# SBUF buffers by the draft's list schedule: a macaron of mixture of experts and routed attention on one core

## The chip, the cores and the metric

The kernel runs on one core of a Trainium2 chip. A core has TensorE (PE, matmuls into PSUM), VectorE (DVE), ScalarE (ACT), GpSimd (POOL) and SyncE (SP, which here issues DMAs); each takes its own instructions strictly in the order in which the program lists them, and semaphores tie the engines together. The metric is device time in microseconds from launch to end. Times are compared by the median of several runs.

## The reference

The input x holds 8 sequences of 1024 rows of 256 numbers. Three layers follow one another, each on a layer norm of its input and added to it:

```
x = x + 0.5 * ffn(layernorm(x))
x = x + attention(layernorm(x))
x = x + 0.5 * ffn(layernorm(x))
```

`ffn` is a mixture of 8 experts, 2 for each row: a router product and softmax choose two experts and their weights, and every expert is `gelu(x @ W1 + b1) @ W2 + b2` with 128 hidden units. `attention` has a light part, 8 heads of 64 in windows of 64 rows that look one window to each side, and a heavy part: two score vectors choose 256 rows for the queries and 256 for the keys of each sequence; these attend to each other fully, and the results are added at the chosen rows.

```
sim = einsum('bhnid,bhnjd->bhnij', qw * scale, kk)      # light: 64 queries, 192 keys
attn = softmax(where(valid, sim, neg))
light_out = einsum('bhnij,bhnjd->bhnid', attn, vv) @ wo_l
hattn = softmax(einsum('bhid,bhjd->bhij', hq * scale, hk))   # heavy: 256 by 256
```

## The kernel before, in words

**Two passes and a planner.** The kernel text (`program`) does not issue instructions. Each call on `nc.tensor`, `nc.vector` and the others records an `Op` (the recording line is L269, so most rows of the profile carry that line). `macaron` runs `program` twice: first as a draft, whose operations `Plan.order` puts into a list order per engine with a model of durations, and then again, emitting them in that order. Copies out of PSUM (`nc.copy`, called `evict`) and scalings may go to either of two engines; the planner chooses.

**How the order is made.** `edges` (L435) collects for each operation what must come before it: operations on the same data, and for buffers that are used again, the users of the earlier tenant. `schedule` (L517) is a list schedule: at every step it takes the engine that can start soonest and the best-ranked ready operation in a window of 40. `backward` (L633) gives ranks from the end; five rounds are run and the best kept.

**Buffers.** SBUF pools such as `two`, `three` and `wpool` hold a fixed count of buffers per tag; `Pool.tile` deals them out in turn in the order in which `program` asks, and `edges` makes all users of one tenant precede all users of the next tenant of that buffer. The four PSUM banks of the pool `pmm` are treated otherwise: `banked` (L319) hands out "loose" tiles, and `schedule` gives such a tile a bank when the first operation that uses it is placed, the bank that has been free for the shortest time. The draft's assignment is then used in the second pass.

**The stages.** `program` builds the work as generators and interleaves their steps by positions along a common axis; `PLACES` holds for each generator (by number) a shift of its start and of its end. The generators:

- `rows`: for a group of one or two sequences, normalise the rows, transpose them (pt), compute the router's logits (pl), rank them, and find a slot for each row in a list sorted by expert, padded to 128 rows per expert; store the rows (y).
- `experts` (L1145): for up to four slots of 128 rows at a time, gather rows (xp, GpSimd), fetch the slot's expert weights (wt, SP), transpose into pt, evict to turned rows xTe, multiply (ph), Gelu to act with 4 x 128 columns for four slots, multiply (po, after a small product that adds b2), evict to yp, and store it to ys.
- `dense` (L1271): for the first and the last sequence all 8 experts are computed for all rows, without gathering: ph, Gelu to act (512 columns for 4 row tiles in the first, 256 for 2 in the last), po, and a weighted sum into the rows on VectorE (x_0at, x_last). The last sequence's four chunks end the program. Each begins with its router: pl, a chain of small VectorE steps to the gate weights, parts, pt_w, turned, and pb.
- `front`, `heavy`, `project`, `light`, `last`: combine the experts' rows, choose rows for the heavy part with eight rounds of digits (pd), compute heavy and light attention, and sum up. A light block: `scores_light` writes sim, `soften` takes the maximum (nmax), exponentials with their sums (a, asum) on ScalarE, the reciprocal, and scales a on VectorE or GpSimd; `keys_first` (L1435) transposes a into pa and evicts it to at; `values_light` (L1523) does the same for pb and bt, multiplies with the values (pav), and evicts to loT, which the output product (lo) reads.

In names, `_2f` is a group of the experts, `_7f` the dense last sequence, `_5atl` light and `_5ath` heavy attention of sequence 5.

**Which buffers take turns.** xTe, yp, bt: two each. at: three. act: two of 4 x 128 columns.

Of the kernel before, what the change touches and what calls it, by code (L numbers as in the profile page):

```python
# [44 lines left out]
F32 = mybir.dt.float32  # L45
# [33 lines left out]
    1: (0.014, 0.072),  # L79
    2: (0.088, 0.002),  # L80
    3: (0.444, -0.124),
    4: (-0.157, -0.245),
    5: (-0.045, -0.526),
    6: (0.377, -0.016),
    8: (-0.109, 0.000),
    9: (0.160, -0.078),
    10: (0.002, -0.129),
    11: (0.070, 0.254),
    12: (0.003, 0.003),
    13: (0.434, 0.082),  # L90
    14: (0.122, -0.024),
    15: (0.274, 0.222),
    16: (0.214, 0.139),
    17: (0.169, 0.000),
    18: (0.273, -0.045),
    19: (0.099, 0.049),
    20: (0.074, -0.435),
    21: (0.000, 0.117),
    22: (0.205, -0.014),
    23: (-0.072, -0.036),  # L100
    24: (-0.039, -0.018),
    25: (-0.013, 0.000),
    26: (0.055, 0.481),
    27: (-0.013, 0.068),
    28: (-0.016, 0.000),
    30: (0.000, 0.002),
    31: (0.000, 0.484),
    32: (0.000, 0.090),
    34: (-0.002, 0.015),
    36: (0.063, 0.000),  # L110
    37: (0.034, -0.012),
    38: (0.032, 0.032),
    39: (0.000, -0.362),
    40: (0.029, 0.010),
    41: (0.499, 0.498),
    42: (0.099, 0.231),
    43: (0.000, 0.020),
    44: (0.050, -0.164),
    45: (0.007, -0.066),
    46: (0.311, 0.028),  # L120
    47: (0.196, 0.228),
    48: (0.076, -0.023),
    49: (0.030, -0.083),
    50: (0.000, 0.068),
    51: (-0.049, -0.114),
    52: (0.025, 0.137),
    53: (0.005, -0.060),
    54: (0.066, -0.609),
    55: (0.019, -0.108),
    56: (0.030, 0.183),  # L130
    57: (0.236, 0.070),
    58: (0.064, 0.043),
    59: (0.047, -0.286),
    60: (0.034, 0.000),
    61: (0.050, 0.000),
    62: (-0.041, -0.014),
    63: (0.123, -0.043),
    64: (-0.124, -0.048),
    65: (-0.290, -0.365),
    66: (-0.097, 0.030),  # L140
    67: (0.024, -0.106),
    68: (-0.011, 0.032),
    69: (0.132, 0.030),
    70: (0.439, 0.061),
# [144 lines left out]
class Plan:  # L289


    def __init__(self, tc, draft=None):
        self.tc, self.nc, self.ops = tc, tc.nc, []
        self.tag = {}
        self.draft = draft
        self.banks = 0
        self.loose = []
        for name in ENGINES:
            setattr(self, name, Engine(self, name))

    def pool(self, ctx, name, bufs, **where):

        made = ctx.enter_context(self.tc.tile_pool(name=name, bufs=1, **where))
        shared, count = name not in ("cons", "dram"), {}

        class Pool:
            @staticmethod
            def tile(shape, dtype, tag, name):
                if shared:
                    count[tag] = count.get(tag, -1) + 1  # L310
                    tag = f"{tag}.{count[tag] % bufs}"
                t = made.tile(shape, dtype, tag=tag, name=name)
                if shared:
                    self.tag[t.name] = tag
                return t

        return Pool

    def banked(self, ctx, name, bufs, **where):  # L319


        made = ctx.enter_context(self.tc.tile_pool(name=name, bufs=1, **where))
        self.banks, ready = bufs, {}

        def make(shape, dtype, tile_name, i):
            return made.tile(shape, dtype, tag=f"{name}.{i}", name=tile_name)

        if self.draft:
            for i, bank in self.draft.opened:
                shape, dtype, tile_name = self.draft.loose[i]  # L330
                ready[i] = make(shape, dtype, tile_name, bank)

        class Pool:
            @staticmethod
            def tile(shape, dtype, name):
                i = len(self.loose)
                self.loose.append((shape, dtype, name))
                if self.draft:
                    assert self.draft.loose[i] == self.loose[i]
                    return ready[i]  # L340
                t = make(shape, dtype, name, 0)
                self.tag[t.name] = i
                return t

        return Pool

# [88 lines left out]
    def edges(self):  # L435
# [42 lines left out]
        for i, users in enumerate(self.users):  # L478
            lo, hi = min(users), max(users)
            down, up = set(users), set(users)  # L480
            for k in range(lo, hi + 1):
                if not before[k].isdisjoint(down):
                    down.add(k)
            for k in range(hi, lo - 1, -1):
                if k in up:
                    up.update(q for q in before[k] if q >= lo)
            inside = users | (down & up)
            asked = set().union(*(before[k] for k in inside)) - inside
            self.asks[i] = len(asked)
            for k in asked:  # L490
                self.opens[k].append(i)
            for k in users:
                self.uses[k].append(i)
# [10 lines left out]
    def in_turn(self, before, result, bank_of):  # L504

        place = {k: i for i, (_, k, _) in enumerate(result)}
        before = [set(qs) for qs in before]
        lines = {}
        for i in sorted(range(len(bank_of)), key=lambda i: min(place[k] for k in self.users[i])):
            lines.setdefault(bank_of[i], []).append(i)  # L510
        for line in lines.values():
            for i, j in zip(line, line[1:]):
                for k in self.users[j]:
                    before[k].update(self.users[i])
        return before

    def schedule(self, before, after, rank):  # L517
# [18 lines left out]
        free_at = dict.fromkeys(range(self.banks), 0.0)  # L536
# [14 lines left out]
        def next_of(e):  # L551

            best, looked = None, 0
            for r, k in waiting[e]:
                how = ops[k].how
                t = max(now[e], ready[k] + SIGNAL[e])
                if self.uses[k]:
                    new = [i for i in self.uses[k] if i not in bank_of]
                    if new:
                        if not free_at or any(asks[i] for i in new):  # L560
                            continue
                        t = max(t, min(free_at.values()) + SIGNAL[e])
# [15 lines left out]
        while len(result) < len(ops):  # L578
            e = min((e for e in ENGINES if found[e]), key=lambda e: found[e][0])
# [27 lines left out]
            for i in self.uses[k]:  # L607
                if i not in bank_of:

                    bank_of[i] = max(  # L610
                        free_at,
                        key=lambda x: (free_at[x] <= t, free_at[x] if free_at[x] <= t else -free_at[x], -x),
                    )
                    del free_at[bank_of[i]]
                last_use[i] = max(last_use[i], done)
                left[i] -= 1
                if not left[i]:
                    free_at[bank_of[i]] = last_use[i]
            if self.opens[k] or self.uses[k]:
                stale.add(PE)  # L620
# [60 lines left out]
    def order(self):  # L681
# [6 lines left out]
        for _ in range(ROUNDS):  # L688
            from_end = self.backward(before, *this[1:])
# [32 lines left out]
def program(  # L722
# [23 lines left out]
    two = nc.pool(ctx, "two", 2)  # L746
    three = nc.pool(ctx, "three", 3)
# [397 lines left out]
    def experts(f, group, routed, results):  # L1145
# [5 lines left out]
        for q in range(0, NS, 4):  # L1151
# [4 lines left out]
            for j in range(0, here, 2):  # L1156
# [16 lines left out]
                pt = bank(f"pt_{m}")  # L1173
                for i in range(two_of):
                    for k in range(KD):
                        nc.tensor.transpose(pt[:, ts(2 * i + k, P)], xp[:, i, ts(k, P)], ident)
                xT = two.tile([P, 2, KD, P], F32, tag="xTe", name=f"xTe_{m}")
# [4 lines left out]
                hidden.append(ph)  # L1182
                for i in range(two_of):
                    for k in range(KD):
                        nc.tensor.matmul(
# [6 lines left out]
            act = two.tile([P, 4, P], F32, tag="act", name=f"act_{n}_{q}")  # L1192
            for i in range(here):
                nc.scalar.activation(act[:, i, :], hidden[i // 2][:, i % 2, :], AF.Gelu, bias=wt[i][:, WROW - 1 : WROW])
            for j in range(0, here, 2):
# [3 lines left out]
                po = bank(f"po_{m}")  # L1199
                for i in range(two_of):  # L1200
                    s = q + j + i
                    nc.tensor.matmul(
# [6 lines left out]
                    nc.tensor.matmul(  # L1209
                        po[:, ts(i, D)],  # L1210
                        act[:, j + i, :],
# [4 lines left out]
                yp = two.tile([P, 2, D], F32, tag="yp", name=f"yp_{m}")  # L1216
# [54 lines left out]
    def dense(rows_of, weights, n, yT=None):  # L1271
# [73 lines left out]
        for e in range(E):  # L1345
            flat = bank(f"ph_{n}_{e}")[:, : m * P]
            for k in range(KD):
                nc.tensor.matmul(
# [6 lines left out]
            act = two.tile([P, 4, P], F32, tag="act", name=f"act_{n}_{e}")  # L1355
            nc.scalar.activation(
                act.rearrange("p i c -> p (i c)")[:, : m * P], flat, AF.Gelu, bias=b1_sb[:, e : e + 1]
            )
            for j in range(0, m, 2):
                po = bank(f"po_{n}_{e}_{j}")  # L1360
                for i in range(2):
                    nc.tensor.matmul(
                        po[:, ts(i, D)],
                        act[:, j + i, :],
# [70 lines left out]
    def keys_first(a, starts, n):  # L1435

        pa = bank(f"pa_{n}")
        for i in range(4):
            k = slice(starts[i % 2], starts[i % 2] + P)
            nc.tensor.transpose(pa[:, ts(i, P)], a[:, i, k], ident)  # L1440
        at = three.tile([P, 4, P], F32, tag="at", name=f"at_{n}")
# [81 lines left out]
    def values_light(a, vside, t, g, loT, n):  # L1523
# [4 lines left out]
        pb = bank(f"pb_{n}_{g}")  # L1528
        for c in range(2):
            pair = a[:, 2 * c : 2 * c + 2, :].rearrange("p j k -> p (j k)")  # L1530
            nc.tensor.transpose(pb[:, ts(c, P)], pair[:, P : 2 * P], ident)
        bt = two.tile([P, 2, P], F32, tag="bt", name=f"bt_{n}_{g}")
# [603 lines left out]
```

## Time and profile before

| | us |
|---|---|
| median of 7 runs | 1834.31 |
| lowest, highest | 1825.64, 1849.82 |
| the profiled execution | 1839.09 |
| its span, first to last instruction | 1837.4 |
| TensorE busy | 1681.8 |
| VectorE busy | 1232.6 |
| ScalarE busy | 917.0 |
| GpSimd busy | 846.6 |
| mean granted TensorE clock | 0.962 |

A row of the profile names line, engine, operation, and the tiles written and read (`out<-in`), then busy time, the mean of one in ns, and the idle time of the engine just before, with what ended it. PEld is the loading of matmul weights, which overlaps PE. "issue" and "remote" are idle times for which the profile shows no releaser of its own. The chain is followed back from the last instruction to what released each step.

### The profile page before, as it was taken

To read this page: it belongs to the slowest core of one execution; us is meant where nothing else is said; L and a number is where in the kernel's file an instruction comes from. 1 tells how busy PE (TensorE), PEld (TensorE's weight loads), DVE (VectorE), ACT (ScalarE), POOL (GpSimd) and SP (SyncE) were. 2 spreads that over 40 slices of the span, in tenths; PEclk is the share of its full clock that TensorE was granted. 3 is DMA by queue.
4 is the path that set the end of the run, shared out by engine and by line. 5 is a ranking of instruction groups with operands and counts; after the bars stand their busy time and mean duration, and the time that the engine had idled before them with its cause. 6 is when DMAs were issued, how large, how long until landed. Compare 5 with 4: busy or idle time off the path is not lost.

```text
span 1837.4 us, 39317 instructions
## 1 busy us (share of the span) xinstructions
PE 1681.8 (92%) x13753; PEld 1255.4 (68%) x13753; DVE 1232.6 (67%) x3904; ACT 917.0 (50%) x2554; POOL 846.6 (46%) x733
## 2 busy tenths in 40 slices
PE   6899899999999998899989899989989998999997
PEld 5576577666766766667667576748757665678786
DVE  5778658863865485677556698649647695558746
ACT  1134446546755543555646345637637554455532
POOL 1054662563643225443555644456445635453433
PEclk8899999999999998999999989999999999999999
DMA  9467664244851235464775432537665525744264
GB/s 157 171 207 220 221 208 146 74 120 140 263 156 55 54 98 172 154 212 122 237 226 173 118 107 87 158 118 228 193 190 165 141 89 164 216 118 132 73 189 125
DMA packets 220134, 284.66 MB, mean 155 GB/s; under 512 B 53496, under 2 KB 160960, under 8 KB 219680
## 3 DMA queue, kind: packets, MB, share of 16 engines
q1 hardware_dynamic: 190992, 208.82, 36.7%
q0 software_dynamic: 28368, 73.31, 15.1%
q8 instruction: 109, 1.79, 0.4%
q14 instruction: 89, 0.73, 0.1%
q10 hardware_dynamic: 576, 0.02, 0.0%
HBM read 196.20 MB, written 80.61 MB: 151 GB/s over the span
## 4 chain that ended last, share of the span: by engine, by line
PE 69%; DVE 16%; issue 5%; ACT 3%; another core or an unknown queue 3%; DMA 3%; POOL 1%; SPq 0%; POOLq 0%; DVEq 0%; ACTq 0%
PE po_0f L269 3%; PE ph_0f L269 2%; PE po_2f L269 2%; PE po_6f L269 2%; PE po_4f L269 2%; PE ph_2f L269 2%; PE po_7f L269 1%; PE ph_6f L269 1%; PE ph_7f L269 1%; PE ph_4f L269 1%; PE pt_2f L269 1%; PE pt_6f L269 1%; PE lk_5at L269 1%; PE pav_5atl L269 1%
## 5 line engine op out<-in xcount | busy, mean ns | idle before, releaser
L269 ACT ACT_TABLE_LOAD x89 | 114.2, 1283 | 2.7 <-DVE nmax_5atl L269 1.2
L269 POOL DMA_INDIRECT xp_2f<-y_2f,token_2f x78 | 82.8, 1062 | 65.8 <-PE pt_2f L269 26.1
L269 POOL DMA_INDIRECT xp_6f<-y_6f,token_6f x62 | 64.4, 1039 | 69.9 <-PE pt_6f L269 43.9
L269 POOL DMA_INDIRECT xp_4f<-y_4f,token_4f x62 | 67.5, 1089 | 41.4 <-PE pt_4f L269 15.3
L269 POOL DMA_INDIRECT xp_0f<-y_0f,token_0f x39 | 41.7, 1069 | 43.7 <-PE pt_0f L269 22.5
L269 PE MATMUL po_2f<-wt_2f,act_2f 128*128 128x256 f32 x156 | 46.7, 391 | 6.1 <-ACT act_2f L269 6.1
L269 PEld LDWEIGHTS ph_2f<-xTe_2f,wt_2f 128*128 128x128 f32 x312 | 42.7, 200 | 8.5 <-issue 5.8
L269 PE MATMUL ph_2f<-xTe_2f,wt_2f 128*128 128x128 f32 x312 | 46.7, 287 | 1.8 <-ACT xTe_2f L352 1.0
L269 PE MATMUL po_0f<-experts,act_0f 128*128 128x256 f32 x128 | 38.1, 441 | 7.4 <-DVE x_0at L269 7.4
L269 POOL DMA_INDIRECT xp_1f<-y_1f,token_1f x23 | 24.7, 1075 | 40.6 <-PE pt_1f L269 14.8
L269 DVE SCALAR_TENSOR_TENSOR x_last<-po_7f,weight_7f,x_last 128x256 f32<-128x256 f32 x64 | 28.4, 479 | 21.8 <-PE po_7f L269 20.2
L269 ACT ACTIVATE act_0f<-ph_0f,b_sb 128x512 f32<-128x512 f32 x16 | 11.0, 687 | 57.4 <-PE ph_0f L269 52.4
L269 PEld LDWEIGHTS po_0f<-experts,act_0f 128*128 128x128 f32 x128 | 27.5, 224 | 17.4 <-DVE x_0at L269 8.2
L377 POOL TENSOR_TENSOR a_7atl<-a_7atl,asum_7atl 128x768 f32<-128x768 f32 x14 | 21.0, 1501 | 40.0 <-DVE asum_7atl L269 21.6
L269 PE MATMUL ph_6f<-xTe_6f,wt_6f 128*128 128x128 f32 x248 | 36.1, 284 | 3.6 <-ACT act_6f L269 3.4
L269 PEld LDWEIGHTS ph_6f<-xTe_6f,wt_6f 128*128 128x128 f32 x248 | 33.3, 196 | 8.3 <-ACT act_6f L269 4.3
L377 POOL TENSOR_TENSOR a_2atl<-a_2atl,asum_2atl 128x768 f32<-128x768 f32 x10 | 14.7, 1473 | 50.4 <-DVE asum_2atl L269 31.9
L269 PE MATMUL po_6f<-wt_6f,act_6f 128*128 128x256 f32 x124 | 35.7, 382 | 1.4 <-issue 1.4
L269 PE MATMUL po_4f<-wt_4f,act_4f 128*128 128x256 f32 x124 | 37.0, 391 | 0.0
L269 PE MATMUL ph_4f<-xTe_4f,wt_4f 128*128 128x128 f32 x248 | 35.9, 279 | 0.4 <-DVE work_6at L269 0.2
L269 PEld LDWEIGHTS ph_4f<-xTe_4f,wt_4f 128*128 128x128 f32 x248 | 32.8, 191 | 5.1 <-issue 2.9
L269 PEld LDWEIGHTS po_2f<-wt_2f,act_2f 128*128 128x128 f32 x156 | 24.4, 196 | 17.2 <-ACT act_2f L269 9.0
(1547 smaller groups left out, 5907.5 us busy)
## 6 DMA issues: line engine op xcount, KB each, us to landing
wt_2f<-wpk SPq DMA_DIRECT2D x78, 256.5 KB
wt_4f<-wpk SPq DMA_DIRECT2D x62, 256.5 KB
wt_6f<-wpk SPq DMA_DIRECT2D x62, 256.5 KB
wt_0f<-wpk SPq DMA_DIRECT2D x39, 256.5 KB
ys_2f<-yp_2f SPq DMA_DIRECT2D x38, 256.0 KB
ys_4f<-yp_4f SPq DMA_DIRECT2D x30, 256.0 KB
ys_6f<-yp_6f SPq DMA_DIRECT2D x30, 256.0 KB
o<-h_b SPq DMA_DIRECT2D x56, 128.0 KB
```

What stands on the lines that cost most here:

```text
L269: op = Op(self.plan, engines, lambda _: issue(*args, **kw), outs, ins, kind, **how)
L377: return getattr(nc, engine).tensor_tensor(dst, dst, by, op=ALU.mult)
```

## The change

The tags xTe, yp, bt, at and act leave the turn: `pool` gets a list `loose` of tags, each of which becomes a `banked` pool of its own in SBUF. The count of buffers and their bytes stay the same; act becomes four buffers of 2 x 128 columns instead of two of 4 x 128, one for each pair of slots or row tiles, so the first dense sequence's 512-wide Gelu becomes two of 256. The schedule keeps free buffers per pool. These SBUF pools are "eager": a buffer is given to a tile when its first user is placed, with no count of what the tile's use still asks for. `room_for` adds the SBUF tile to the inputs that the planner sees of the TensorE operations which fill the PSUM bank that will be evicted into it, so that the planner begins such a product only when both a bank and a buffer are there; the emitted instruction does not read it. If no operation can be placed, the schedule counts as endless. Most entries of `PLACES` also change, so that the whole program is ordered anew.

```diff
 PLACES = {
     0: (-0.182, -0.019),
-    1: (0.014, 0.072),
-    2: (0.088, 0.002),
-    3: (0.444, -0.124),
+    1: (-0.281, -0.011),
+    2: (-0.160, 0.002),
+    3: (0.733, -0.124),
...
-    70: (0.439, 0.061),
+    70: (0.463, 0.085),
 }
...
+    def room_for(self, op, room):
+
+        op.ins = op.ins + [room]
...
         for i, users in enumerate(self.users):
+            if self.loose[i][0] in self.eager:
+                for k in users:
+                    self.uses[k].append(i)
+                continue
...
-        free_at = dict.fromkeys(range(self.banks), 0.0)
+        free_at = {pool: dict.fromkeys(range(n), 0.0) for pool, n in self.banks.items()}
+        pool_of = [loose[0] for loose in self.loose]
...
-                        if not free_at or any(asks[i] for i in new):
+                        pools = [pool_of[i] for i in new]
+                        if any(asks[i] for i in new) or any(
+                            len(free_at[x]) < pools.count(x) for x in pools
+                        ):
                             continue
...
             if self.opens[k] or self.uses[k]:
-                stale.add(PE)
+                stale.update(ENGINES)
...
-    two = nc.pool(ctx, "two", 2)
-    three = nc.pool(ctx, "three", 3)
+    two = nc.pool(ctx, "two", 2, loose=("xTe", "yp", "bt"))
+    three = nc.pool(ctx, "three", 3, loose=("at",))
+    four = nc.pool(ctx, "four", 4, loose=("act",))
...
+                xT = two.tile([P, 2, KD, P], F32, tag="xTe", name=f"xTe_{m}")
                 for i in range(two_of):
                     for k in range(KD):
-                        nc.tensor.transpose(pt[:, ts(2 * i + k, P)], xp[:, i, ts(k, P)], ident)
-                xT = two.tile([P, 2, KD, P], F32, tag="xTe", name=f"xTe_{m}")
+                        o = nc.tensor.transpose(pt[:, ts(2 * i + k, P)], xp[:, i, ts(k, P)], ident)
+                        nc.room_for(o, xT)
...
-            act = two.tile([P, 4, P], F32, tag="act", name=f"act_{n}_{e}")
-            nc.scalar.activation(
-                act.rearrange("p i c -> p (i c)")[:, : m * P], flat, AF.Gelu, bias=b1_sb[:, e : e + 1]
-            )
+                for act in acts:
+                    nc.room_for(o, act)
+            for j, act in enumerate(acts):
+                nc.scalar.activation(
+                    act.rearrange("p i c -> p (i c)"),
+                    flat[:, ts(j, 2 * P)],
+                    AF.Gelu,
+                    bias=b1_sb[:, e : e + 1],
+                )
...
     def keys_first(a, starts, n):
 
         pa = bank(f"pa_{n}")
+        at = three.tile([P, 4, P], F32, tag="at", name=f"at_{n}")
         for i in range(4):
             k = slice(starts[i % 2], starts[i % 2] + P)
-            nc.tensor.transpose(pa[:, ts(i, P)], a[:, i, k], ident)
-        at = three.tile([P, 4, P], F32, tag="at", name=f"at_{n}")
+            nc.room_for(nc.tensor.transpose(pa[:, ts(i, P)], a[:, i, k], ident), at)
         evict(at.rearrange("p i q -> p (i q)"), pa)
         return at
```

## The prediction

> **What bounds the kernel now.** I read the page first (busy shares, the granted clock, the chain), then the longest waits of the matmul engine, then a table of stretches, then the timeline at the three largest of those waits, and last the rows of the tiles that the change touches. The page's first two parts:
>
> ```profile
> span 1837.4 us, 39317 instructions
> PE 1681.8 (92%) x13753; PEld 1255.4 (68%) x13753; DVE 1232.6 (67%) x3904; ACT 917.0 (50%) x2554; POOL 846.6 (46%) x733
> ...
> PEclk8899999999999998999999989999999999999999
> ...
> PE 69%; DVE 16%; issue 5%; ACT 3%; another core or an unknown queue 3%; DMA 3%; POOL 1%; SPq 0%; POOLq 0%; DVEq 0%; ACTq 0%
> ...
> L269 ACT ACT_TABLE_LOAD x89 | 114.2, 1283 | 2.7 <-DVE nmax_5atl L269 1.2
> ```
>
> TensorE is busy for 1682 of 1837 us and carries 69% of the chain. No other engine is near its limit, so a change of order can win only what TensorE now loses: its idle time, 152 us when the gaps between its matmuls are added up, and the granted clock below 1. Its waits, longest first (who waited, for whom, us in total, times, longest):
>
> ```profile
> PE pt_0f L269 <- DVE y_0f L269: 8.7, 1, 8.7
> PE po_0f L269 <- DVE x_0at L269: 7.4, 1, 7.4
> PE pt_1f L269 <- issue: 6.1, 1, 6.1
> PE po_2f L269 <- ACT act_2f L269: 6.1, 2, 5.2
> PE pt_7f_w L269 <- DVE parts_7f L269: 4.9, 1, 4.9
> ...
> PE pav_5atl L269 <- ACT act_4f L269: 4.2, 1, 4.2
> ...
> PE ph_6f L269 <- ACT act_6f L269: 3.4, 2, 2.7
> ```
>
> Grouped over all its rows, this idle time is 47 us "issue" (many gaps under 1 us at changes of matmul shape), 20.8 us in 14 waits that end on a Gelu (act), 9.5 us on turned probabilities (at), 8.0 us on loT, 3.9 us on turned rows (xTe), 3.3 us on bt, 2 us on yp, and some 57 us on twenty other kinds. Of the five buffers that the change frees, only Gelu's results cost much. By stretch (busy us of PE, PEld, DVE, ACT, POOL, then clock, DMA share, GB/s):
>
> ```profile
> 0.00:100.00 100.00, 76.42 (x316) 55.83 (x317) 67.23 (x280) 17.68 (x27) 15.85 (x34) 0.85 0.64 154
> ...
> 800.00:900.00 100.00, 98.32 (x807) 75.41 (x806) 61.01 (x192) 55.57 (x140) 40.97 (x34) 1.00 0.56 165
> 1000.00:1100.00 100.00, 89.99 (x727) 64.24 (x726) 75.53 (x197) 41.55 (x139) 56.67 (x46) 0.93 0.42 121
> ```
>
> The first 100 us hold 24 us of the idle time. The timeline at three places:
>
> ```profile
> 65.43 0.43 DVE L269 BATCH_NORM_STATS2 st_2f<-rows_2f 128x6 f32<-128x256 f32 x1 [7.48 <-DMA rows_2f<-in_x]
> 67.31 2.08 PE L269 MATMUL po_0f<-experts,act_0f 128*128 128x256 f32 x4 [7.41 <-DVE x_0at L269]
> ...
> 1200.86 0.62 ACT L269 ACTIVATE act_2f<-ph_2f,wt_2f 128x128 f32<-128x128 f32 x2 [5.13 <-remote]
> ...
> 1818.09 0.66 PE L269 MATMUL pt_7f_w<-ident,parts_7f 128*96 128x128 f32 x2 [4.85 <-DVE parts_7f L269]
> ```
>
> At 65 us VectorE stood in order behind statistics of rows that had not landed, and the sums that free the po banks stood behind those. At 1200 us ScalarE itself stood still for 5 us with no cause that the trace shows. At 1818 us the last chunk had no matmul left to do beside VectorE's gate chain.
>
> **The change, part by part.** The program's order follows from the plan, so I compared the order of instructions of both built programs. Work is the same: 8284 matmul instructions and 753 separate weight loads, 559 DMAs issued on POOL and 881 on SP, in both. It does what it says: consecutive yp tiles share a buffer 42 times instead of 4. What moves, with distances counted as matmul time between two instructions in TensorE's order (0.215 us per 256-column pass, from the timeline's back-to-back starts):
>
> - **Gelu to second product.** From the last ph product to the first po product that reads its Gelu the median distance grows from 2.6 to 4.7 us in the sparse experts (148 pairs) and from 2.1 to 3.9 us in the dense ones (64); what is missing to 2 us falls from 53 to 22 us. Against the 14 waits (20.8 us, the largest 5.23, 4.19, 2.73) two more microseconds of cover leave about 6 us: bounds 0 (ScalarE's standstills land where the cover is thin) and -15. I take -9.
> - **Last chunk.** Between the router's products pl and the turning pt_7f_w stood three experts' steps; now seven, since four half-size Gelu buffers let four ph run ahead where two did. Each step is 0.86 us (ph starts at 1803.90, po at 1804.76): 3.4 us of the 4.85 us are covered. Bounds 0 and -4.85; -3.4. Next late there is the gate chain itself.
> - **Start.** VectorE's statistics of rows_2f still stand in order: ahead of the sums of the dense half's experts 5 to 7 now, of 6 and 7 before. On SP the load of rows_2f still follows both stores of rows_1f, which follow the attention weights. So the 7.41 us wait stays, perhaps an expert's step longer (+1.7 us). In exchange the first sparse group's slot arithmetic, tiled and spot now stand before that wait, not behind it, and its expert numbers and weight fetches on SP before the store of rows_2f and the load of rows_3f, which queue behind them; on the chain the first gather xp_1f follows at 117 us. Bounds -7.4 and +1.7; -2.
> - **loT.** The distance from pav to the output product, short of 2 us by 85 us in all, is short by 55: of 8.0 us of waits, -3 (0 to -8). The distances of xTe, at and bt are level at their short ends, so 0 there: their waits of 3.9, 9.5 and 3.3 us stay.
> - **yp.** The nearest reuse of a buffer moves from 2.6 to 4.6 us of matmuls, so a store hardly holds an eviction: 0, beside yp's 2 us.
> - **Split Gelu.** Sixteen 512-wide Gelus of 687 ns become thirty-two of 473 ns: 16 x (946 - 687) = +4.1 us on ScalarE, which waits 56.5 us for ph there; the first half is ready 0.2 us sooner, 16 x 0.214 = 3.4 us. Bounds -3.4 to +4.1; 0, covered by that idle time.
> - **Function tables.** 96 loads stand in the program instead of 90: 6 x 1.283 = 7.7 us on an engine that is 50% busy and holds 3% of the chain. Share on the path 0.06, so +0.5; bounds 0 and +7.7.
> - **Copies and scalings.** Ten copies go from ScalarE (585 ns) to VectorE (691 ns), 6.9 us on an engine with 605 us free; four 1024-wide scalings go to POOL and four 768-wide ones to VectorE. Hidden, 0; without cover they cost those 7 us.
> - **Attention is tighter.** From the last score matmul of a light block to the first turning of its probabilities the median falls; blocks with under 7 us between go from 9 to 21 of 128, under 8 us from 17 to 33. The chain in between is maximum 0.948, four exponentials and their sums 4 x (0.431 + 0.217), reciprocal 0.172, scaling 0.948 on VectorE or 1.555 on POOL: 4.7 to 5.3 us without queueing. For 12 more blocks under 7 us: 0 to 1.3 us each, 0 to +16; I take +4, nearer the low end since the waits on POOL's scaling are 2.3 us in all now.
> - **Clock.** The clock's missing 0.038 is spread like the idle time (0.85 where 24 us are idle, 1.00 where under 2 us are). With some 13 of 152 us gone: bounds 0 and -7; -2.
>
> The sum is -9 - 3.4 - 2 - 3 + 0.5 + 4 - 2 = -14.9 us against this execution's own 1839.09 us (1.7 us outside its span): 1824. The execution lies 0.26% above the median of the seven times, 1834.31; on the median the forecast is 1819, 0.8% less.
>
> [...]
>
> **The rivals.**
> - **The squeeze decides (slower).** What is won elsewhere is paid back where attention was packed closer: the 33 light blocks under 8 us wait for their scaled probabilities. Without the +4 the sum is -18.9 us, so the change is lost at 0.57 us a block and slower by over 0.5% at 0.85. For it: scalings on POOL queue behind row gathers of 1.06 us each. Against it: only 9 of 128 blocks lie under 6 us, and the waits on POOL's scaling are 2.3 us now. I price it at 1 us a block, 33 us: 1848.
> - **The waits were never about buffers (same).** ScalarE stands still six times for 5 to 7 us on "remote" or "issue" (the row at 1200.86 is one), and most of the act idle time is that. If it lands elsewhere unchanged, only the last chunk's 3.4 us and the 3 us at loT remain: 1828.
> - **More moves than I count (faster).** The 57 us of other waits and the clock come from the same queues in order; if a third of them goes too, about 22 us more: 1797.
> - That the buffers still go in turn is excluded by the 42 pairs above.
>
> **How the numbers follow.** Measurement tells about 0.5% from no change (the seven times spread from 1825.64 to 1849.82). Forecast case 0.41, more moves 0.14, same 0.23, squeeze 0.22. Faster by over 0.5% (below 1825.1) is 0.41 + 0.14 = 0.55, same 0.23, slower 0.22. The likeliest case alone, by the bounds of the Gelu term (6 us either way) and of the start, runs from 1808 to 1825. The range over all cases goes from the third less 6 us, 1791, to the squeeze and 2 us more, 1850; what lies outside is the tail of either.
>
> **What would show it.** Right: TensorE's idle time near 138 us, act waits under 10 us, a first gather xp_1f earlier than 117 us, pt_7f_w waiting under 2 us, 95 table loads in the trace, the mean clock at or above 0.963. Wrong: pa and pb waiting for POOL's or VectorE's scaled probabilities in many places (the squeeze), or act waits as large as before beside ScalarE idle on "remote". A standstill of ScalarE or a late row load at a new place would make it wrong without saying anything of the buffers.

## The result and the profile after

The changed kernel takes 1872.14 us in the median of 19 runs, beside 1835.96 us for the kernel before in 46 runs: a ratio of 1.0197, 95% interval 1.0176 to 1.0218. It is 2% slower, and outside the range that was forecast.

The page of the changed kernel, in the same parts as before:

```profile
span 1871.9 us, 39332 instructions
PE 1696.0 (91%) x13753; PEld 1262.1 (67%) x13753; DVE 1232.8 (66%) x3913; ACT 929.3 (50%) x2567; POOL 851.6 (45%) x733
...
PEclk8899999999989999999998999999989999899999
...
PE 63%; DVE 18%; issue 8%; DMA 4%; another core or an unknown queue 3%; ACT 3%; POOL 1%; ACTq 0%; SPq 0%; POOLq 0%; DVEq 0%
...
L271 ACT ACT_TABLE_LOAD x95 | 121.9, 1283 | 26.2 <-issue 10.2
```

The span grew by 34.5 us. TensorE is busy 14.2 us longer with the same 13753 matmuls, and not busy 20.3 us longer. The first part is the clock: the stretches at half clock add up to 142.4 us before and 170.2 us after, and half of the difference is 13.9 us (sixteen products pl_2f took 1.93 us at 79.36 us of before, at clock 1.00, and 3.58 us at 82.59 us, at 0.50). So the question is where the new idle time is. The longest waits of TensorE (who waited, for whom, us in total, times, longest):

```profile
PE pt_0f L271 <- DVE y_0f L271: 8.6, 1, 8.6
PE pt_0f L271 <- DVE x_0at L271: 8.4, 1, 8.4
PE lo_2at L271 <- DVE loT_3at_l L366: 6.2, 1, 6.2
PE pt_7f_w L271 <- DVE parts_7f L271: 4.7, 2, 4.1
...
PE pt_1f L271 <- DVE rows_1f L271: 4.4, 1, 4.4
...
PE pr_0at L271 <- DVE taken_0at L271: 3.5, 1, 3.5
PE ph_4f L271 <- DVE work_2at L271: 3.5, 1, 3.5
PE sim_1atl L271 <- DVE asum_1atl L271: 3.4, 1, 3.4
PE pt_1f L271 <- DMA xp_1f<-y_1f,token_1f: 3.3, 2, 2.1
```

No Gelu stands among them. Grouped over all rows, before and after: act 20.8 to 1.8 us; loT 8.0 to 18.2; the digits of the choice (work) 5.0 to 11.6; best and taken 0.3 to 7.4; rows 0 to 5.0; "issue" 46.9 to 52.5; sums of exponentials (asum) 0.1 to 4.2; at 9.5 to 4.1; kT 4.1 to 0.8. The 19 us at act are gone, and more than that is spread over other releasers. The same stretches as in the table of before, and the timeline at the largest new wait and at two places that the prediction named (the start, and the last chunk's gate chain from lg to parts):

```profile
0.00:100.00 100.00, 73.34 (x307) 55.19 (x308) 65.96 (x271) 19.06 (x36) 25.64 (x40) 0.83 0.72 180
...
800.00:900.00 100.00, 87.32 (x642) 65.72 (x643) 55.34 (x180) 43.94 (x108) 35.95 (x30) 0.91 0.52 150
1000.00:1100.00 100.00, 90.12 (x652) 64.62 (x651) 54.36 (x136) 50.69 (x136) 57.23 (x52) 0.91 0.54 161
```

```profile
68.28 1.12 PE L271 MATMUL pt_0f<-ident,y_0f 128*128 128x128 f32 x4 [8.40 <-DVE x_0at L271]
...
865.09 1.11 PE L271 MATMUL lv_3at<-wqkv_sb,xT_3at 128*128 128x512 f32 x2
...
868.82 0.42 DVE L366 COPY loT_2at_l<-pav_2atl 128x256 f32<-128x256 f32 x1 [3.25 <-remote]
...
871.88 0.42 DVE L366 COPY loT_3at_l<-pav_3atl 128x256 f32<-128x256 f32 x1 [2.63 <-remote]
...
872.36 1.22 PE L271 MATMUL lo_2at<-wol_sb,loT_2at_l 128*128 128x256 f32 x2 [6.15 <-DVE loT_3at_l L366]
...
1843.04 0.17 DVE L271 TENSOR_TENSOR lg_7f<-pl_7f,rb_sb 128x16 f32<-128x16 f32 x1
...
1853.40 0.61 PE L271 MATMUL pt_7f_w<-ident,parts_7f 128*96 128x128 f32 x2 [4.14 <-DVE parts_7f L271]
```

The stretch from 800 to 900 us, where before was 98% busy at full clock, shows the loss best. At 865 us the products pav_2atl and pav_3atl had been recorded as ended (the last at 865.0), TensorE did two more matmuls, and then nothing for 6 us, because the output product waits for loT, and loT's copies wait on "remote". What those copies need is only TensorE's own signal that pav is done. It came 3.8 and 6.9 us after that end.

That can be counted. For each signal of TensorE in the trace I took the time since the end of the last matmul that carries one; delays over 0.8 us, those within 3 us of each other taken as one with its longest, and the program's end left out. Before there are 53 such **standstills** with 99.7 us, after 67 with 132.2 us: 32.5 us more (other ways of pairing a signal with a matmul give 100 to 105 us before and 128 to 138 after). A standstill here is a late signal. Whether TensorE itself stands is not shown: the records have it at work in part of these stretches, and without a matmul for some 55 us of them before and 73 us after. Those 18 us are nearly all of the 18.7 us by which the gaps between TensorE's matmuls grew (151.7 to 170.4); with the 13.9 us of clock they come near the 34.5 us of the span. The 5.13 us in the row at 1200.86 of before, put down to ScalarE in the prediction, is one of them: it is TensorE's signal for ph that was late.

### The profile page after: what moved, and what is told of

The parts are those of the page before. It is cut to its first block, busy times and chain, and to the rows that moved or that the text cites. A ratio compares the mean times of both kernels' runs of the same rounds, so it can differ in the third digit from the quotient of the medians.

```text
span 1871.9 us, 39332 instructions
## 1 busy us (share of the span) xinstructions
PE 1696.0 (91%) x13753; PEld 1262.1 (67%) x13753; DVE 1232.8 (66%) x3913; ACT 929.3 (50%) x2567; POOL 851.6 (45%) x733
## 4 chain that ended last, share of the span: by engine, by line
PE 63%; DVE 18%; issue 8%; DMA 4%; another core or an unknown queue 3%; ACT 3%; POOL 1%; ACTq 0%; SPq 0%; POOLq 0%; DVEq 0%
PE po_0f L271 2%; PE po_2f L271 2%; PE po_4f L271 2%; PE ph_2f L271 2%; PE ph_0f L271 1%; PE ph_4f L271 1%; PE po_6f L271 1%; PE ph_6f L271 1%; PE ph_7f L271 1%; PE po_7f L271 1%; PE pt_2f L271 1%; PE pav_5atl L271 1%; PE pt_6f L271 1%; PE lo_5at L271 1%
## 5 line engine op out<-in xcount | busy, mean ns | idle before, releaser
L271 ACT ACT_TABLE_LOAD x95 | 121.9, 1283 | 26.2 <-issue 10.2
L271 ACT ACTIVATE act_0f<-ph_0f,b_sb 128x256 f32<-128x256 f32 x32 | 13.4, 471 | 52.1 <-PE ph_0f L271 52.1
L271 POOL DMA_INDIRECT xp_5f<-y_5f,token_5f x23 | 24.6, 1070 | 25.6 <-PE pt_5f L271 18.9
L391 POOL TENSOR_TENSOR a_1atl<-a_1atl,asum_1atl 128x768 f32<-128x768 f32 x8 | 11.8, 1479 | 51.2 <-DVE asum_1atl L271 32.1
L271 DVE SCALAR_TENSOR_TENSOR x_0at<-po_0f,weight_0f,x_0at 128x256 f32<-128x256 f32 x64 | 28.2, 477 | 9.6 <-PE po_0f L271 9.3
```

The source lines that it names most:

```text
L271: op = Op(self.plan, engines, lambda _: issue(*args, **kw), outs, ins, kind, **how)
L391: return getattr(nc, engine).tensor_tensor(dst, dst, by, op=ALU.mult)
```

## The experiments

**Theories.** A: the loose buffers and the early claim on them (`room_for`) cost the time. B: the new entries of `PLACES` cost it. C: any new order of the same work lands some tens of us from the old one; its form S, after the first runs: what differs are the standstills that fall on an order.

**E1 to E4: the two halves, and two nudges.** E1 is the kernel before with the change's table `PLACES`, E2 the changed kernel with the old one. E3 and E4 are the kernel before and the changed kernel with entry 14 nudged:

```diff
# E1, and the reverse in E2; the whole table of the change
-    1: (0.014, 0.072),
+    1: (-0.281, -0.011),
...
# E3 and E4
-    14: (0.122, -0.024),
+    14: (0.124, -0.024),
```

> The kernel before with the new entries of PLACES and its buffers in turn as they were. Theory A (the loose buffers and the early claim on them cost the time): a ratio of 0.995 to 1.005 to the kernel before. Theory B (the new positions cost it): 1.015 to 1.025, as the whole change, with TensorE idle near 170 us. Theory C (any new order of the same work lands some tens of us from the old one, whatever its buffers): a ratio that neither the new positions nor the buffers explain by themselves, so the two halves of the change don't add up to 1.020; here anything from 1.00 to 1.04.

> The changed kernel with the old entries of PLACES: the buffers, the halved Gelu and the early claim alone. Theory A: 1.015 to 1.025. Theory B: 0.985 to 1.005, Gelu waits of TensorE under 10 us in all and the gain of my prediction (about 15 us) on the chip. Theory C: between 1.00 and 1.03, with the Gelu waits small as in the whole change and the loss spread over many other releasers.

> The kernel before with one entry of PLACES (number 14, start) shifted by 0.002, buffers in turn; the first part of the order is the same, later parts are ordered anew. Theories A and B: 0.997 to 1.006, since nothing of the change is in it. Theory C: the same kind of loss as the whole change without any of its parts, 1.01 or more, TensorE idle 10 us or more above the 152 us of before and more half-clock stretches.

> The changed kernel with one entry of PLACES (number 14, start) shifted by 0.002. Theories A and B: 1.015 to 1.025 to the kernel before, like the whole change, since all its parts are in it. Theory C: another value, more than 0.5% from the changed kernel on either side.

These four ran on a chip where the kernel before takes 1694.83 us, not 1836. Ratios to it: E1 (positions alone) 1.0141 (1.0077 to 1.0205), E2 (buffers alone) 0.9969 (0.9938 to 1.0001), E3 1.0035 (1.0007 to 1.0064), E4 1.0098 (1.0069 to 1.0127). E4 lies below what A and B gave it and more than 0.5% from the changed kernel's 1.0197, as C asked; but that was measured on other chips. Page, longest "issue" wait and Gelu waits of E3, which has before's buffers and much of before's order (the same matmuls up to 349 us, and in all 83% at the same place in TensorE's order):

```profile
span 1698.3 us, 39339 instructions
...
PE 1618.9 (95%) x13753; PEld 1224.5 (72%) x13753; DVE 1237.1 (73%) x3905; ACT 924.5 (54%) x2559; POOL 851.5 (50%) x733
```

```profile
PE pt_1f L269 <- issue: 4.9, 1, 4.9
...
PE pt_2f L269 <- ACT act_2f L269: 0.6, 1, 0.6
...
PE pt_2f L269 <- ACT act_0f L269: 0.4, 1, 0.4
PE lq_0at L269 <- ACT act_2f L269: 0.3, 1, 0.3
```

On this chip there is no standstill in any of the four traces, stretches at half clock add up to 55 to 91 us, and TensorE waits 1.8 us in all for Gelu with the buffers in turn (E3; 1.6 in E1) and 0 and 1.2 us with loose ones (E2, E4). So the 20.8 us at act were not the price of buffers in turn: without standstills there is hardly anything there to win. The same holds for the 47 us of "issue", which the prediction put down to changes of matmul shape: in E3, with the same work and much of the order, the row above is all of it. Theory A falls (E2), and B gains: positions alone cost 1.4% without any standstill. Each half is a new order, though: 16% of TensorE's matmuls stand at the same place as before in E1, 17% in E2. So B rests on the new positions being slower each time that they are run, and C isn't excluded. E1's trace shows one way. Two short waits of TensorE, and the stretch around them in E1 and then in E3:

```profile
1016.75 1.40 PE L271 MATMUL sim_4ath<-hbuf_4at 64*128 64x256 f32 x8 [2.31 <-DVE junk_5at L271]
...
1019.41 1.12 PE L271 MATMUL pt_3f<-ident,rows_3f 128*128 128x128 f32 x4 [1.27 <-DVE rows_3f L271]
```

```profile
1000.00:1050.00 50.00, 45.80 (x383) 34.45 (x381) 42.38 (x126) 25.01 (x87) 12.31 (x7) 0.86 0.28 83
```

```profile
1000.00:1050.00 50.00, 46.61 (x425) 32.70 (x424) 49.70 (x173) 25.89 (x84) 16.25 (x9) 1.00 0.17 56
```

In E1 the clock is halved from 1017.5 on for 13.7 us, which costs, as an estimate from half of that time, 6.8 us on top of the 3.6 us of waits. In all E1 has 91 us at half clock and E3 60; half of the difference is 15.4 of the 19.9 us that its matmuls take longer, and 13 us more of gaps make the rest of the 33 us between their spans. But E1's profiled execution is the slowest of its four (1732.85 us, median 1722.70), at a clock of 0.974 where the others have 0.980 to 0.982; the medians of E1 and E3 are 20.8 us apart. How much of that is clock this trace doesn't tell.

**E5 and E6: both kernels again.**

> The changed kernel itself once more. The last four runs were on a chip where the kernel before takes 1695 us, not 1836, and where TensorE's semaphores come on time: of 2000 only the artefact at the end comes over 1 us after its matmul, against 87 (before) and 106 (after) in the two traces of the result; Gelu waits are 1.8 us with the buffers in turn. Theory S (the 2% are standstills of TensorE, which fell on the changed order harder): on a chip without standstills the ratio is 0.990 to 1.005, since e2 is 0.997 and positions as new as these were placed for these buffers; on a chip with standstills again 1.015 to 1.025. Theory B (the new positions): 1.010 to 1.020 on either, near e1's 1.014.

> The kernel before, for a trace on the same chip as e5. Theory S on a chip without standstills: act waits of TensorE under 3 us where the trace of before had 20.8, TensorE idle 70 to 80 us, 8 to 11 half-clock stretches instead of 25. With standstills: late semaphores over 1 us near 87 again, and the question is whether they come at the same matmuls (sim_6atl at 1536, po_2f at 1201, po_4f at 1375) or at others.

This was a chip with standstills again (before 1837.88 us). E5: 1.0128 (1.0082 to 1.0175). So E5 does not tell S from B, but the two traces show what a standstill belongs to. The place at 865 us, in E5:

```profile
862.28 0.42 DVE L366 COPY loT_2at_l<-pav_2atl 128x256 f32<-128x256 f32 x1 [3.26 <-remote]
...
865.33 0.42 DVE L366 COPY loT_3at_l<-pav_3atl 128x256 f32<-128x256 f32 x1 [2.62 <-remote]
...
865.80 1.65 PE L271 MATMUL lo_2at<-wol_sb,loT_2at_l 128*128 128x256 f32 x3 [6.17 <-DVE loT_3at_l L366]
```

The same waits to some hundredths of a us, in another execution. By place in TensorE's order (within 40 instructions), 61 of the 67 standstills of the changed kernel recur in E5, and 44 of before's 53 in E6; against a list shifted by 1500 instructions 9 and 4 do. E6's Gelu waits are 10.4 us, not under 3: with the standstills they are back, at half of the 20.8 us that the same kernel's first trace had.

**E7 to E10: the halves on a chip with standstills, and another order of before.** E7 is the changed kernel, E8 the kernel of E2, E9 that of E1. E10 is the kernel before with

```diff
-    8: (-0.109, 0.000),
+    8: (-0.113, -0.015),
...
-    26: (0.055, 0.481),
-    27: (-0.013, 0.068),
+    26: (0.033, 0.508),
+    27: (-0.014, 0.082),
...
-    59: (0.047, -0.286),
+    59: (0.054, -0.306),
```

> The changed kernel beside the two halves of the change on one chip. In the two traces of it so far TensorE's late semaphores come at the same matmuls (8 of the 10 longest in both), 138 and 136 us in all against 104 and 109 for the kernel before: the standstills belong to a chip and an order together. Theory S: on a chip with standstills 1.010 to 1.022; on one without, 0.990 to 1.005. Theory B (positions): 1.010 or more on both.

> Old positions, new buffers, as e2 (0.997 on a chip without standstills). Theory S on a chip with standstills: the ratio is 0.997 plus what its late semaphores hold above the 107 us of the kernel before, so each 18 us of them more is 1%; 0.99 to 1.03, and the trace says which. If the new buffers themselves bring the standstills (theory A): 1.010 to 1.022 with late semaphores near 137 us. On a chip without, 0.994 to 1.000 again.

> New positions, buffers in turn, as e1 (1.014 on a chip without standstills). Theory S on a chip with standstills: 1.014 plus 1% for each 18 us of late semaphores above 107 us. If the new positions bring the standstills (theory B): near 1.03, late semaphores near 137 us. On a chip without, 1.008 to 1.020 again.

> The kernel before with four entries of PLACES (8, 26, 27, 59) moved by at most 0.03, buffers in turn: nothing of the change, another order. Theory C/S (the chip's standstills fall on any new order in their own way): on a chip with standstills a ratio between 0.99 and 1.03 that goes with the sum of its late semaphores, and other matmuls than sim_2atl near 760 and sim_6atl near 1536 among its longest where the order differs. On a chip without, 0.998 to 1.008. Theories A and B: 1.00 on both.

Before takes 1831.81 us here. E7 1.0205 (1.0152 to 1.0258), E8 1.0034 (0.9990 to 1.0078), E9 1.0287 (1.0247 to 1.0327), E10 0.9956 (0.9919 to 0.9994). Theory B again, for both kinds of buffers, and A falls again as an explanation of the 2%. E9 is E1's kernel, and its Gelu waits are 15.5 us here beside E1's 1.6. But E10, which has nothing of the change in it, moves the time too, and its standstills are 74.7 us. E10's page:

```profile
span 1814.3 us, 39346 instructions
...
PE 1671.6 (92%) x13753; PEld 1250.0 (69%) x13753; DVE 1227.5 (68%) x3884; ACT 914.8 (50%) x2566; POOL 853.2 (47%) x737
```

**E11 and E12: another order of the changed kernel.** E11 is the changed kernel, E12 moves four of its entries by at most 0.03:

```diff
-    27: (-0.013, 0.068),
+    27: (0.013, 0.069),
...
-    60: (0.030, -0.111),
+    60: (0.044, -0.097),
...
-    63: (0.128, -0.038),
+    63: (0.108, -0.008),
...
-    66: (0.047, 0.296),
+    66: (0.068, 0.268),
```

> The changed kernel, beside e12. On a chip with standstills of TensorE (late semaphores 130 us in all, half-clock stretches 162 to 170 us, against 100 to 105 and 142 to 149 for the kernel before): 1.012 to 1.022, as three times before. On a chip without: if the standstills make the loss, 0.990 to 1.005; if the new positions make it, 1.008 or more.

> The changed kernel with four entries of PLACES (27, 60, 63, 66) moved by at most 0.03: the buffers and nearly all of the new positions, in another order from the first group on. If every order of this buffering has more standstills (the buffers' doing): 1.010 to 1.025 on a chip with standstills, late semaphores 125 us or more. If it is this one order's bad luck with this kind of chip: anywhere from 0.995 to 1.025, likeliest 1.005, with late semaphores of 75 to 130 us. On a chip without standstills 0.995 to 1.010.

With standstills again (before 1861.69 us): E11 1.0163 (1.0098 to 1.0227), E12 1.0213 (1.0153 to 1.0272) with 137 us of standstills. The likeliest value that I gave for E12, 1.005, missed: this small move did not leave the bad neighbourhood.

**E13 to E16: which entries.** E13 and E14 are the changed kernel with the new entries for one part of the stages and the old ones for the rest; E15 is E10's kernel and E16 the changed one.

```diff
# E13: entries 25 to 65 as before
-    26: (0.225, 0.549),
+    26: (0.055, 0.481),
...
# E14: entries 0 to 24 and 66 to 70 as before
-    1: (-0.281, -0.011),
+    1: (0.014, 0.072),
...
```

> The changed kernel with the new entries of PLACES only for the rows, experts, sums and dense stages (0 to 24 and 66 to 70); attention's entries (25 to 65) are the old ones. Old entries throughout gave 1.003, new ones throughout 1.016 to 1.021 on chips with standstills. If the loss sits in the positions of the experts' stages: 1.012 to 1.025 here and below 1.008 in e14. If it belongs to no group of entries but to orders as a whole: both between 1.00 and 1.025, not adding up.

> The counterpart: new entries for attention alone (25 to 65), old ones for the rest. If the loss sits in attention's positions: 1.012 to 1.025 here and below 1.008 in e13, and the lag against e8 grows between 15% and 55% of TensorE's work, as it does in the changed kernel.

> The kernel of e10 again (four entries moved by at most 0.03, buffers in turn), which was 0.9956 of the kernel before. If a good order is good on every chip with standstills: 0.992 to 0.999; if it was one chip's chance: 0.999 to 1.008. On a chip without standstills: 0.998 to 1.006.

> The changed kernel, in case this chip has no standstills, which is the one comparison missing: 0.990 to 1.005 if standstills make the whole loss, 1.008 or more if the new positions make it by themselves. On a chip with standstills 1.012 to 1.022 again.

Before takes 1838.35 us. E13 (experts' entries new) 1.0116 (1.0056 to 1.0176), E14 (attention's new) 1.0043 (1.0012 to 1.0073), E16 1.0215 (1.0165 to 1.0265). Above E8's 1.0034 these are 0.8% and 0.1%, while both together give 1.7 to 1.8% (E7, E16, on the same chip): more of it goes with the experts' positions, but no group carries it alone. E15 is 0.9918 (0.9885 to 0.9952), on the same chip as E10, so whether it would hold on another chip is open. It is the one kernel here that beats both, and it does so with the old buffers.

**E17 and E18: the buffers under a third set of positions.** E17 is the changed kernel with E10's `PLACES`: the old table and the four entries shown there.

> The changed kernel's buffers, halved Gelu and early claim with the positions of e10 (the old ones with four entries moved by at most 0.03), a third set of positions under both kinds of buffers. In turn these positions gave 0.996 and 0.992. If the buffers are worth nothing or little either way beside the order: a ratio between 0.99 and 1.01. If they gain by themselves (a reading of e9 against the changed kernel, 1.029 to 1.020): 0.980 to 0.988, which would beat both kernels.

> The changed kernel, for the one comparison still missing. On a chip without standstills 0.990 to 1.005 if they make the whole loss, 1.008 or more if the new positions do; on a chip with them 1.012 to 1.022 again.

Before takes 1853.31 us. E17 1.0105 (1.0067 to 1.0143), E18 1.0178 (1.0138 to 1.0218). So the loose buffers cost 1.5 to 1.9% on E10's positions (E10 and E15 ran on another chip than E17), 0.3% (uncertain by 0.4) on the old ones, and gain 0.7 to 1.6% on the new ones, where E9 has 1.0287 (0.7 and 0.8% on E9's own chip). Their sign depends on the order they land in; a worth of their own is not to be read off.

All traces from chips with standstills, us of the profiled execution (one execution each; standstills to some 8 us by the pairing, half clock to 2 us by what the end cuts off):

| kernel | span | standstills | at half clock |
|---|---|---|---|
| before; E6 | 1837; 1844 | 100; 105 | 142; 149 |
| E10; E15: before, four entries moved | 1814; 1831 | 75; 90 | 119; 133 |
| E8: old positions, new buffers | 1842 | 126 | 157 |
| E17: E10's positions, new buffers | 1872 | 111 | 174 |
| E9: new positions, buffers in turn | 1880 | 126 | 183 |
| changed kernel: the result, E5, E7, E16, E11, E18 | 1872, 1860, 1868, 1873, 1884, 1894 | 132, 131, 131, 120, 124, 131 | 170, 160, 162, 163, 177, 197 |
| E12: changed, four entries moved | 1884 | 137 | 164 |
| E13; E14: part of the new positions | 1849; 1845 | 110; 98 | 162; 129 |

Over these 16 traces the span rises by 1.05 us for each us of standstills (correlation 0.84); it goes with the time at half clock more closely (0.91). These are correlations; no run took the standstills alone away. Their sum alone doesn't set the time either: E8 and E9 ran on one chip with 126 us each, and their spans are 38 us apart.

## Why the prediction was wrong

- **Gelu to second product (-9).** The waits went as forecast and further (act 20.8 to 1.8 us). The step that failed is reading them as what the order between ph and po costs: "two more microseconds of cover leave about 6 us". E3 shows that with buffers in turn they are 1.8 us where TensorE's signals come on time. They were the places where late signals landed: five of the 14 waits, 16.0 of the 20.8 us, end 0.3 to 0.7 us after one. In the new order these land on loT (+10 us) and others. The "issue" time was misread in the same way: 47 us with the standstills, 4.9 us in E3 without. The rival "the waits were never about buffers" had this mechanism, and named ScalarE where it is TensorE. Its price, 1828, took the standstills as a fixed amount; they rose from 100 to about 130 us.
- **The new positions.** The sum has no term for them. I compared distances for the five freed buffers and let every other wait "stay" or cost nothing, though most entries of `PLACES` change and the whole order with them. E1 and E9 measure that omission at +1.4% and +2.9% with the buffers in turn; E13 and E14 show no single group behind it. This is the step that gave the wrong side; how the new order loses the time is shown only in part. TensorE's gaps, forecast near 138 us, went from 151.7 to 170.4.
- **loT (-3).** The counted distances grew, and the waits rose from 8.0 to 18.2 us, with the standstill at 865 us the largest part (6.15 us): without standstills, in E3, they are 2.0 us.
- **Clock (-2).** The term was +13.9 us: half of 27.8 us more at half clock. The -2 took the clock's loss to go with the idle time, as an estimate of mine between its bounds; no run shows that gain. In the 3.4 us before the stretch in E1 TensorE has 2.31 us of gaps, in the 3.4 us before the one at 82.05 us of the kernel before only 0.23 us, and there a gap of 2.65 us up to 1551.4 us is followed by none (clock 1.00 from 1548 to 1556). So idle time alone doesn't foretell the halving.
- **Last chunk (-3.4).** -0.7: 4.14 us remain of 4.85. The cover came: from the router's product pl to the turning of the gates there are 11.4 us now (1841.97 to 1853.40) and were 8.6 (1809.52 to 1818.09). But the gate chain behind it, from lg to the turning, takes 10.4 us (1843.04) instead of 7.5 (1810.59), since six sums x_last (0.48 us each) stand in it on VectorE instead of two, from the additional experts' steps, and VectorE waits 0.92 us there for a load of o. The term took the chain's length as given.
- **Start (-2).** The first turning of gathered rows moved from 113.1 to 77.5 us, as forecast, and the wait on x_0at grew from 7.41 to 8.40, inside its bounds. But TensorE did 73.34 us of work in the first 100 us instead of 76.42: the gain did not show.
- **Attention tighter (+4).** Waits on the scaled probabilities and their sums went from 2.4 to 5.9 us, near the +4 by luck: those on the scaled probabilities, which the term is about, fell from 2.3 to 1.8, and 3.4 us of the rest is one wait (sim_1atl for asum_1atl) at a standstill of 3.1 us. The squeeze is not what made the kernel slower.
- **Function tables.** 95 loads, as forecast; the idle time before them rose from 2.7 to 26.2 us, off the chain (ACT 3% in both).
- **The likeliest case's range.** By the stated bounds of the Gelu term (9 us above -9) and of the start (3.7 us above -2) its upper end is 1832, not 1825. The measured 1872 lies far above either.

**What stays open.** What a standstill is; how an order of the same work comes to more of them, or to more time at half clock; whether the changed kernel itself loses anything on a chip without them (it never came to run on one; its nearest relatives there are E4 with 1.0098 and E2 with 0.9969); and whether the standstills cause the difference between orders or share its cause, since E1 loses 1.4% without any.

## What to carry to other kernels

Before pricing a wait, ask whether its releaser is late by the order or by the machine: a row that ends on "remote", or a consumer that waits for a product recorded as ended, may mark lateness that a new order puts elsewhere and doesn't remove, as here from act to loT. And where an edit brings a retuned table of an order along, try the table and the edit apart, and one or two nudges of the old table too: here moves of 0.03 in four entries were worth 0.4 to 0.8% on one chip, as much as the edit could have been.

## What the runs showed of the hardware

- Chips differ: the kernel before took 1695 us on one and 1832 to 1862 on the others (1838 and 1853 in two rounds on one of them). On the slower ones TensorE's signals come late at some 40 to 70 places, 75 to 137 us in all; on the faster one never, the program's end left out. Most standstills recur at the same place in the order (61 of the changed kernel's 67 in E5, 44 of before's 53 in E6): the two waits of 3.25 and 2.63 us at loT came as 3.26 and 2.62, 3.23 and 2.63, 3.26 and 2.62 in E5, E7 and E16, though not in E11 and E18.
- The traces with standstills also lack signals: 1865 of TensorE's 2031 are recorded in the changed kernel's and 1882 of 2074 in before's, but 2019 of 2021 in E4's, which has no standstill. What ties the missing signals to the late ones no run shows.
- In the traces of before and after the half-clock stretches are whole multiples of 3.4 us (3.4, 6.8, 10.2, 13.7, 17.1) but for the one that the trace's end cuts off. In E1 the 13.7 us that follow a wait of 2.31 us cost 6.8 us, as an estimate from half of that time: more than the wait. Not every stretch follows such a wait (before's at 82.05 us has 0.23 us of gaps in the 3.4 us ahead of it).
